# Seven 256-cubed products in place of each 512-cubed product in a two-layer graph network, float32

## The chip, the cores and the metric

The kernel runs on one core of a Trainium2 chip. The metric is the device time of one execution in microseconds (us), the median of several runs. Five engines of the core work side by side, each through its own queue in order: TensorE (PE in the profile, with its weight loads as PEld), VectorE (DVE), ScalarE (ACT), GpSimd (POOL) and SyncE (SP). They meet through semaphores. Sixteen DMA engines move the data.

## The reference

There are 32 independent batches of 512 nodes with 512 features, one adjacency matrix for all, and two layers. Cut to what matters:

```python
# x: (32, 512, 512), adj: (512, 512), all float32
def reference(x, adj, W0, b0, Wq, bq, Wk, bk, Wv, bv, Wo, bo):
    h = jnp.maximum(_layernorm(x), 0.0)
    x = x + jnp.einsum('nm,bmd->bnd', adj, h) @ W0 + b0          # layer 0
    h = jnp.maximum(_layernorm(x), 0.0)                          # layer 1: attention, 8 heads
    q, k, v = heads(h @ Wq + bq), heads(h @ Wk + bk), heads(h @ Wv + bv)
    scores = q @ k.T / 8 + (1.0 - adj) * -1000000000.0
    return x + merge(softmax(scores) @ v) @ Wo + bo
```

The mask term of layer 1 uses a weighted adjacency matrix, so in each row the largest entry of `adj` is ahead of the next by far more than any score. The softmax is then 1 at that place and 0 elsewhere, and the attention is a gather of one row. The kernel tests on the chip whether this holds and takes one of two branches. With the inputs here it takes the gathered branch, `single_path`. That branch needs three 512x512x512 products for each batch: `adj @ h`, then that times `W0`, and `h1 @ (Wv Wo)`; then row `idx[n]` of the last is added to row `n` of `x`.

## The kernel before, in words

A matrix of 512 rows lies in SBUF as 128 partitions by 4 chunks by 512 columns. A TensorE matmul takes a 128x128 block as weights and streams up to 512 columns. One 512-cubed product is 4 output chunks of 4 accumulating matmuls, 128x512 each, into one PSUM bank (pool `ps_m`, 5 banks; pool `ps_t`, 3 banks, is for transposes). In float32 each such matmul leaves two records in the trace, so a product shows as 32 records.

For every batch `b`:

- `ln0(b)` computes the first layer norm and ReLU: VectorE statistics (L163, L164, L166, L170), a power of -0.5 on GpSimd (L168, `rstd`), the scaling with ReLU on ScalarE (L172) into `h0`; GpSimd then adds the bias of layer 0 to `x` (L178).
- `aggregate(b)`, L185: the product of `h0` with the transposed adjacency matrix `adjT`; ScalarE copies it to `yT` (L186).
- `layer0(b)`, L192: the product of `yT` with `w0_s`; VectorE adds it onto `x` (L193), and `norm_relu` makes `h1` from it.
- `layer1(b)`: 16 transposes of `h1` on TensorE (L203), copied by VectorE to `h1T` (L204); the product with the folded weights `wvo` (L208), to which VectorE adds the row `cvo` (L210); the result goes to DRAM as `z` (L211, a DMA issued by ScalarE), an indirect DMA of GpSimd adds the picked rows onto `x` (L213), and SyncE's queue stores `x` (L216).

The outer loop runs `layer0(b)`, `aggregate(b + 1)`, `ln0(b + 2)`, `layer1(b)`. So TensorE's work of one round is 32 records of L192, 32 of L185, 16 transposes and 32 of L208, and while it runs `aggregate(b + 1)` the other engines make `h1` of batch `b`. Nothing in the code fixes the order on an engine: a scheduler of the tile framework places each instruction into its engine's queue ahead of time, and pools (`xpool` 5 batches, `work` 2 buffers a name) decide when a buffer can be written again. A queue is strictly in order at run time.

The folding of the weights (`fold_weights`, L142 to L157) is done once, in the first round. The other branch, `general_path`, is not run with these inputs and is not touched.

Of the kernel before, what the change touches and what calls it, by code (L numbers as in the profile page):

```python
# [8 lines left out]
F32 = mybir.dt.float32  # L9
I32 = mybir.dt.int32  # L10
U32 = mybir.dt.uint32
AF = mybir.ActivationFunctionType
ALU = mybir.AluOpType
AX = mybir.AxisListType
PSUM = bass.MemoryType.PSUM
DRAM = bass.MemoryType.DRAM

P = 128
# [6 lines left out]
def gnn_two_layers(ctx: ExitStack, tc: tile.TileContext, x, adj, w0, b0, wq, bq, wk, bk, wv, bv, wo, bo, out):  # L25
# [66 lines left out]
    with tc.If(single > P - 1) as cmp:  # L92
        single_path(tc, x, w0, b0, wv, bv, wo, bo, out, adjT, idx, ident, ones)
# [3 lines left out]

@with_exitstack
def single_path(ctx: ExitStack, tc: tile.TileContext, x, w0, b0, wv, bv, wo, bo, out, adjT, idx, ident, ones):
    nc = tc.nc  # L100
    B, N, D = x.shape
    C, DC = N // P, D // P

    consts = ctx.enter_context(tc.tile_pool(name="consts", bufs=1))
    xpool = ctx.enter_context(tc.tile_pool(name="xpool", bufs=5 * C))
    work = ctx.enter_context(tc.tile_pool(name="work", bufs=2))
    small = ctx.enter_context(tc.tile_pool(name="small", bufs=4))
    ps_m = ctx.enter_context(tc.tile_pool(name="ps_m", bufs=5, space=PSUM))
    ps_t = ctx.enter_context(tc.tile_pool(name="ps_t", bufs=3, space=PSUM))
    dram = ctx.enter_context(tc.tile_pool(name="dram", bufs=3, space=DRAM))  # L110

    X, H0, YT, H1, Z = {}, {}, {}, {}, {}

    def load_x(b):
        for c in range(C):
            X[b, c] = xpool.tile([P, D], F32, name="x")
            nc.sync.dma_start(X[b, c], x[b, c * P:(c + 1) * P, :])  # L117

    load_x(0)
    w0_s = consts.tile([P, DC, D], F32, name="w0_s")  # L120
    nc.sync.dma_start(w0_s, w0.rearrange("(c p) o -> p c o", p=P))
    b0_r = consts.tile([P, D], F32, name="b0_r")
    nc.gpsimd.dma_start(b0_r, bass.AP(tensor=b0.tensor, offset=b0.offset, ap=[[0, P], [1, D]]))
    load_x(1)
    mhalf = consts.tile([P, C], F32, name="mhalf")
    nc.gpsimd.memset(mhalf, -0.5)
    wvo = consts.tile([P, DC, D], F32, name="wvo")
    cvo = consts.tile([P, D], F32, name="cvo")

    def fold_weights():  # L130
        with ExitStack() as tmp:
            fold = tmp.enter_context(tc.tile_pool(name="fold", bufs=1))
            wv_s = fold.tile([P, DC, D], F32, name="wv_s")
            nc.scalar.dma_start(wv_s, wv.rearrange("(c p) o -> p c o", p=P))
            wo_s = fold.tile([P, DC, D], F32, name="wo_s")
            nc.scalar.dma_start(wo_s, wo.rearrange("(c p) o -> p c o", p=P))
            bv_c = fold.tile([P, DC], F32, name="bv_c")
            nc.gpsimd.dma_start(bv_c, bv.rearrange("(c p) -> p c", p=P))
            nc.gpsimd.dma_start(cvo, bass.AP(tensor=bo.tensor, offset=bo.offset, ap=[[0, P], [1, D]]))
            wvT = fold.tile([P, DC, D], F32, name="wvT")  # L140
            for j in range(DC):
                pt = ps_t.tile([P, DC, P], F32, name="pt")  # L142
                for i in range(DC):
                    nc.tensor.transpose(pt[:, i, :], wv_s[:, i, j * P:(j + 1) * P], ident)  # L144
                nc.scalar.copy(wvT[:, j, :], pt.rearrange("p c q -> p (c q)"))
            for i in range(DC):
                ps = ps_m.tile([P, D], F32, name="mm")
                for j in range(DC):
                    nc.tensor.matmul(ps, wvT[:, j, i * P:(i + 1) * P], wo_s[:, j, :], start=(j == 0), stop=(j == DC - 1))  # L149
                nc.scalar.copy(wvo[:, i, :], ps)  # L150
            part = fold.tile([P, D], F32, name="part")
            nc.vector.tensor_scalar_mul(part, wo_s[:, 0, :], bv_c[:, 0:1])
            for j in range(1, DC):
                nc.vector.scalar_tensor_tensor(part, wo_s[:, j, :], bv_c[:, j:j + 1], part, op0=ALU.mult, op1=ALU.add)
            ps = ps_m.tile([P, D], F32, name="mm")
            nc.tensor.matmul(ps, ones, part, start=True, stop=True)
            nc.vector.tensor_add(cvo, ps, cvo)  # L157

    def norm_relu(b, dst):
        mv = small.tile([P, C, nc.vector.BN_AGGR_DIM], F32, name="mv")  # L160
        for c in range(C):
            st = small.tile([P, nc.vector.BN_STATS_DIM], F32, name="st")
            nc.vector.bn_stats(st, X[b, c])  # L163
            nc.vector.bn_aggr(mv[:, c, :], st)  # L164
        ve = small.tile([P, C], F32, name="ve")
        nc.vector.tensor_scalar_add(ve, mv[:, :, 1], EPS)  # L166
        rstd = small.tile([P, C], F32, name="rstd")
        nc.gpsimd.tensor_tensor(rstd, ve, mhalf, ALU.pow)  # L168
        off = small.tile([P, C], F32, name="off")
        nc.vector.scalar_tensor_tensor(off, mv[:, :, 0], -1.0, rstd, op0=ALU.mult, op1=ALU.mult)  # L170
        for c in range(C):
            nc.scalar.activation(dst[:, c, :], X[b, c], AF.Relu, bias=off[:, c:c + 1], scale=rstd[:, c:c + 1])  # L172

    def ln0(b):
        H0[b] = work.tile([P, C, D], F32, name="h0")
        norm_relu(b, H0[b])
        for c in range(C):
            nc.gpsimd.tensor_add(X[b, c], X[b, c], b0_r)  # L178

    def aggregate(b):  # L180
        YT[b] = work.tile([P, DC, N], F32, name="yT")
        for d in range(DC):
            ps = ps_m.tile([P, N], F32, name="mm")
            for m in range(C):
                nc.tensor.matmul(ps, H0[b][:, m, d * P:(d + 1) * P], adjT[:, m, :], start=(m == 0), stop=(m == C - 1))  # L185
            nc.scalar.copy(YT[b][:, d, :], ps)  # L186

    def layer0(b):
        for c in range(C):
            ps = ps_m.tile([P, D], F32, name="mm")  # L190
            for d in range(DC):
                nc.tensor.matmul(ps, YT[b][:, d, c * P:(c + 1) * P], w0_s[:, d, :], start=(d == 0), stop=(d == DC - 1))  # L192
            nc.vector.tensor_add(X[b, c], ps, X[b, c])  # L193
        H1[b] = work.tile([P, C, D], F32, name="h1")
        norm_relu(b, H1[b])

    def layer1(b):
        h1T = work.tile([P, DC, N], F32, name="h1T")
        Z[b] = dram.tile([N, D], F32, name="z")
        for c in range(C):  # L200
            pt = ps_t.tile([P, DC, P], F32, name="pt")
            for d in range(DC):
                nc.tensor.transpose(pt[:, d, :], H1[b][:, c, d * P:(d + 1) * P], ident)  # L203
            nc.vector.tensor_copy(h1T[:, :, c * P:(c + 1) * P], pt)  # L204
        for c in range(C):
            ps = ps_m.tile([P, D], F32, name="mm")
            for d in range(DC):
                nc.tensor.matmul(ps, h1T[:, d, c * P:(c + 1) * P], wvo[:, d, :], start=(d == 0), stop=(d == DC - 1))  # L208
            zs = work.tile([P, D], F32, name="zs", bufs=C)
            nc.vector.tensor_add(zs, ps, cvo)  # L210
            nc.scalar.dma_start(Z[b][c * P:(c + 1) * P, :], zs)  # L211
        for c in range(C):
            nc.gpsimd.indirect_dma_start(  # L213
                out=X[b, c], out_offset=None, in_=Z[b],
                in_offset=bass.IndirectOffsetOnAxis(ap=idx[:, c, 0:1], axis=0), compute_op=ALU.add)
            nc.sync.dma_start(out[b, c * P:(c + 1) * P, :], X[b, c])  # L216

    ln0(0)
    aggregate(0)
    if B > 1:  # L220
        ln0(1)
    for b in range(B):
        if b + 2 < B:
            load_x(b + 2)
        layer0(b)
        if b == 0:
            fold_weights()
        if b + 1 < B:
            aggregate(b + 1)
        if b + 2 < B:  # L230
            ln0(b + 2)
        layer1(b)
# [265 lines left out]
```

## Time and profile before

| what | us |
|---|---|
| median of 3 runs | 1471.41 (1471.16 to 1471.71) |
| the profiled execution, own time | 1469.63 |
| its span, first to last instruction | 1467.5 |
| TensorE busy in the span | 1407.2 (96%) |
| VectorE busy | 484.4 (33%) |
| GpSimd busy | 430.1 (29%) |
| ScalarE busy | 265.4 (18%) |
| mean granted TensorE clock | 0.991 |

The span is the part of the execution that the profile covers; the 2.1 us between it and the execution's own time lie around it. Busy time of TensorE is a sum over records, which overlap: a record of a 128x512 float32 matmul lasts 0.592 us while the next one starts 0.429 us after it. So the pitch from start to start says how fast the stream runs, and not the duration. The other four engines are busy for a third of the span at most, but a small share of busy time doesn't say whether an engine answers soon enough, nor what stands in front of an instruction in its queue.

### The profile page before, as it was taken

Reading aid. Unit: us, or ns where it says so; the run is one execution under the profiler, and the core shown is the slowest. Engines: PE = TensorE matmul, PEld = TensorE weight load, DVE = VectorE, ACT = ScalarE, POOL = GpSimd, SP = SyncE. Lnnn points to the kernel's source line nnn. Section 1 sums busy time; section 2 is a strip of 40 time slices with the busy share of each in tenths; the row PEclk is TensorE's granted clock in tenths of the full one; section 3 lists DMA queues with packets and bytes.
Section 4 is the critical chain, followed back from the end, with each engine's and each line's share of the span. In section 5 each row is a group of like instructions: output and inputs, shape, how many; then the busy total and the mean of one; then the engine's idle time right before and its main releaser. Section 6 shows DMA issues by size and latency. Waiting matters only on the chain.

```text
span 1467.5 us, 10607 instructions
## 1 busy us (share of the span) xinstructions
PE 1407.2 (96%) x3654; PEld 652.3 (44%) x3654; DVE 484.4 (33%) x1051; ACT 265.4 (18%) x405; POOL 430.1 (29%) x333
## 2 busy tenths in 40 slices
PE   2899999999999999999999999999999999999984
PEld 1344444444444444444444444444444444444441
DVE  2323332333342333333233333323333433333231
ACT  2222102222211222210122221022222112222100
POOL 1313223233323323332322332232333233233111
PEclk9999999999999999999999999999999999999997
DMA  5404432333443234343224344323334422333333
GB/s 175 155 8 108 115 82 79 98 101 101 115 115 72 80 102 105 101 115 100 73 86 107 101 107 115 84 77 98 100 101 115 114 66 88 105 74 72 86 86 89
DMA packets 77216, 141.85 MB, mean 97 GB/s; under 512 B 8416, under 2 KB 8416, under 8 KB 77152
## 3 DMA queue, kind: packets, MB, share of 16 engines
q0 software_dynamic: 18688, 34.09, 15.1%
q1 hardware_dynamic: 37920, 69.22, 13.6%
q10 hardware_dynamic: 20544, 37.76, 6.8%
q8 instruction: 31, 0.51, 0.1%
q14 instruction: 33, 0.27, 0.1%
HBM read 73.93 MB, written 67.11 MB: 96 GB/s over the span
## 4 chain that ended last, share of the span: by engine, by line
PE 95%; DMA 2%; DVE 1%; POOL 0%; ACT 0%; issue 0%; SPq 0%; POOLq 0%; ACTq 0%
PE mm L185 30%; PE mm L208 30%; PE mm L192 30%; PE pt L203 4%; PE mm L149 1%; DMA x<-in_x_dram 1%; DMA wt<-in_L_gnn_Wk_dram 1%; POOL x L213 0%; DVE idx L73 0%; DVE top L72 0%; DMA z<-zs 0%; SPq L117 0%; ACT wt L60 0%; POOLq L493 0%; ACT h L172 0%
## 5 line engine op out<-in xcount | busy, mean ns | idle before, releaser
L185 PE MATMUL mm<-adjT,h 128*128 128x512 f32 x1024 | 446.6, 594 | 7.0 <-ACT h L172 7.0
L208 PE MATMUL mm<-wvo,h1T 128*128 128x512 f32 x1024 | 445.9, 593 | 0.0
L192 PE MATMUL mm<-w_s,yT 128*128 128x512 f32 x1024 | 444.7, 592 | 0.0
L213 POOL DMA_INDIRECT x<-z,idx x128 | 201.0, 1570 | 702.2 <-DMA z<-zs 631.1
L185 PEld LDWEIGHTS mm<-adjT,h 128*128 128x128 f32 x1024 | 195.2, 191 | 253.0 <-issue 238.1
L192 PEld LDWEIGHTS mm<-w_s,yT 128*128 128x128 f32 x1024 | 194.6, 190 | 244.9 <-issue 244.9
L208 PEld LDWEIGHTS mm<-wvo,h1T 128*128 128x128 f32 x1024 | 192.2, 190 | 229.2 <-issue 229.1
L186 ACT COPY yT<-mm 128x512 f32<-128x512 f32 x128 | 74.2, 580 | 1042.2 <-DVE st L163 937.2
L172 ACT ACTIVATE h<-x,off,rstd 128x512 f32<-128x512 f32 x256 | 187.5, 803 | 77.3 <-DVE off L170 74.8
L210 DVE TENSOR_TENSOR zs<-mm,cvo 128x512 f32<-128x512 f32 x128 | 88.5, 691 | 341.0 <-PE mm L208 341.0
L193 DVE TENSOR_TENSOR x<-mm,x 128x512 f32<-128x512 f32 x128 | 88.5, 692 | 269.7 <-PE mm L192 269.7
L163 DVE BATCH_NORM_STATS2 st<-x 128x6 f32<-128x512 f32 x256 | 172.4, 683 | 15.7 <-DMA x<-in_x_dram 11.3
L178 POOL TENSOR_TENSOR x<-x,b_r 128x512 f32<-128x512 f32 x128 | 159.2, 1276 | 52.0 <-ACT h L172 48.3
L204 DVE COPY h1T<-pt 128x512 f32<-128x512 f32 x128 | 79.6, 683 | 250.7 <-PE pt L203 250.7
L168 POOL TENSOR_TENSOR rstd<-ve,mhalf 128x4 f32<-128x4 f32 x64 | 65.5, 1024 | 250.1 <-DVE mv L164 188.5
L203 PE MATMUL pt<-ident,h 128*128 128x128 f32 x512 | 68.1, 276 | 4.3 <-ACT h L172 4.2
L203 PEld LDWEIGHTS pt<-ident,h 128*128 128x128 f32 x512 | 57.9, 142 | 29.3 <-issue 23.3
L164 DVE BATCH_NORM_AGGREGATE mv<-st 128x2 f32<-128x6 f32 x256 | 40.4, 173 | 3.5
L170 DVE SCALAR_TENSOR_TENSOR off<-mv,rstd 128x4 f32<-128x4 f32 x64 | 10.4, 163 | 55.0 <-POOL rstd L168 55.0
L149 PE MATMUL mm<-wo_s,wvT 128*128 128x512 f32 x32 | 13.9, 592 | 0.0
L67 PE MATMUL pt<-ident,mask 128*128 128x128 f32 x16 | 3.9, 426 | 10.0 <-DMA mask<-in_adj_dram 10.0
L144 PE MATMUL pt<-ident,wv_s 128*128 128x128 f32 x16 | 3.6, 423 | 8.3 <-DMA wv_s<-in_L_gnn_Wv_dram 8.3
(44 smaller groups left out, 56.9 us busy)
## 6 DMA issues: line engine op xcount, KB each, us to landing
x<-in_x_dram SPq DMA_DIRECT2D x128, 256.0 KB, 3.5
z<-zs ACTq DMA_DIRECT2D x128, 256.0 KB, 2.0
out_dram<-x SPq DMA_DIRECT2D x128, 256.0 KB, 3.9
x<-z,idx POOLq DMA_INDIRECT x128, 5.9
wt<-in_L_gnn_Wq_dram ACTq DMA_DIRECT2D x1, 1024.0 KB, 9.8
mask<-in_adj_dram SPq DMA_DIRECT2D x1, 1024.0 KB, 9.2
wt<-in_L_gnn_Wk_dram ACTq DMA_DIRECT2D x1, 1024.0 KB, 11.9
wv_s<-in_L_gnn_Wv_dram ACTq DMA_DIRECT2D x1, 1024.0 KB, 7.4
```

The costliest lines, as they stand in the source:

```text
L163: nc.vector.bn_stats(st, X[b, c])
L172: nc.scalar.activation(dst[:, c, :], X[b, c], AF.Relu, bias=off[:, c:c + 1], scale=rstd[:, c:c + 1])
L178: nc.gpsimd.tensor_add(X[b, c], X[b, c], b0_r)
L185: nc.tensor.matmul(ps, H0[b][:, m, d * P:(d + 1) * P], adjT[:, m, :], start=(m == 0), stop=(m == C - 1))
L186: nc.scalar.copy(YT[b][:, d, :], ps)
L192: nc.tensor.matmul(ps, YT[b][:, d, c * P:(c + 1) * P], w0_s[:, d, :], start=(d == 0), stop=(d == DC - 1))
L193: nc.vector.tensor_add(X[b, c], ps, X[b, c])
L203: nc.tensor.transpose(pt[:, d, :], H1[b][:, c, d * P:(d + 1) * P], ident)
L204: nc.vector.tensor_copy(h1T[:, :, c * P:(c + 1) * P], pt)
L208: nc.tensor.matmul(ps, h1T[:, d, c * P:(c + 1) * P], wvo[:, d, :], start=(d == 0), stop=(d == DC - 1))
L210: nc.vector.tensor_add(zs, ps, cvo)
L213: nc.gpsimd.indirect_dma_start(out=X[b, c], out_offset=None, in_=Z[b], in_offset=bass.IndirectOffsetOnAxis(ap=idx[:, c, 0:1], axis=0), com ...
```

## The change

Each of the three products in a batch is computed by Strassen's scheme in Winograd's form. Both operands are seen as 2x2 blocks of 256x256. Instead of 8 block products there are 7, and sums of blocks are formed before and after. The constant operands (`adjT`, `w0_s`, `wvo`) get their four sums once (`sums_b`); the operand that changes with the batch gets them each time (`sums_a`: four additions of 128 partitions by 512 elements). For `h0` they are on GpSimd, for `yT` and `h1T` on VectorE. A block product is 4 matmuls of 128x256 in one PSUM bank (`gemm`); three of the seven stay in the bank `u` and one more in `v`, so that partial sums are accumulated by TensorE, and each of the seven is read by one instruction after it has ended: by VectorE where it is added onto what is there, by ScalarE where it is only copied.

Around this: `aggregate` becomes a generator, and the transposes of `h1`, now a function of their own, are placed after its fourth block product. Their copies go from VectorE to ScalarE. The row `cvo` is no longer added to `z`, but to `x`, four additions on GpSimd in each round. `norm_relu` of layer 0's result is done in two halves. `ps_m` has 6 banks and `ps_t` 2; `work` has one buffer a name but for `h0` and its sums; `xpool` holds 4 batches.

```diff
--- before.py
+++ after.py
@@ -97,24 +97,108 @@
 
 @with_exitstack
 def single_path(ctx: ExitStack, tc: tile.TileContext, x, w0, b0, wv, bv, wo, bo, out, adjT, idx, ident, ones):
     nc = tc.nc
     B, N, D = x.shape
     C, DC = N // P, D // P
+    HALF = N // 2
 
     consts = ctx.enter_context(tc.tile_pool(name="consts", bufs=1))
-    xpool = ctx.enter_context(tc.tile_pool(name="xpool", bufs=5 * C))
-    work = ctx.enter_context(tc.tile_pool(name="work", bufs=2))
+    xpool = ctx.enter_context(tc.tile_pool(name="xpool", bufs=4))
+    work = ctx.enter_context(tc.tile_pool(name="work", bufs=1))
     small = ctx.enter_context(tc.tile_pool(name="small", bufs=4))
-    ps_m = ctx.enter_context(tc.tile_pool(name="ps_m", bufs=5, space=PSUM))
-    ps_t = ctx.enter_context(tc.tile_pool(name="ps_t", bufs=3, space=PSUM))
+    ps_m = ctx.enter_context(tc.tile_pool(name="ps_m", bufs=6, space=PSUM))
+    ps_t = ctx.enter_context(tc.tile_pool(name="ps_t", bufs=2, space=PSUM))
     dram = ctx.enter_context(tc.tile_pool(name="dram", bufs=3, space=DRAM))
 
-    X, H0, YT, H1, Z = {}, {}, {}, {}, {}
+    X, H0, H0S, YT, YTS, H1, H1T, H1TS, Z = {}, {}, {}, {}, {}, {}, {}, {}, {}
 
     def load_x(b):
-        for c in range(C):
-            X[b, c] = xpool.tile([P, D], F32, name="x")
-            nc.sync.dma_start(X[b, c], x[b, c * P:(c + 1) * P, :])
+        X[b] = xpool.tile([P, C, D], F32, name="x")
+        for c in range(C):
+            nc.sync.dma_start(X[b][:, c, :], x[b, c * P:(c + 1) * P, :])
+    def blk(t, chunks, cols):
+        return t[:, 2 * chunks:2 * chunks + 2, cols * HALF:(cols + 1) * HALF]
+    def sums_a(eng, t, name, bufs=1):
+        s = work.tile([P, 4, 2, HALF], F32, name=name, bufs=bufs)
+        a11, a12, a21, a22 = blk(t, 0, 0), blk(t, 1, 0), blk(t, 0, 1), blk(t, 1, 1)
+        eng.tensor_add(s[:, 0], a21, a22)
+        eng.tensor_sub(s[:, 1], s[:, 0], a11)
+        eng.tensor_sub(s[:, 2], a11, a21)
+        eng.tensor_sub(s[:, 3], a12, s[:, 1])
+        return s
+    def sums_b(eng, t, name):
+        s = consts.tile([P, 4, 2, HALF], F32, name=name)
+        b11, b12, b21, b22 = blk(t, 0, 0), blk(t, 0, 1), blk(t, 1, 0), blk(t, 1, 1)
+        eng.tensor_sub(s[:, 0], b12, b11)
+        eng.tensor_sub(s[:, 1], b22, s[:, 0])
+        eng.tensor_sub(s[:, 2], b22, b12)
+        eng.tensor_sub(s[:, 3], b21, s[:, 1])
+        return s
+    def product(a, sa, bt, sb, take):
+        def gemm(bank, lhs, rhs, first):
+            for m in range(2):
+                for k in range(2):
+                    nc.tensor.matmul(bank[:, m, :], lhs[:, k, m * P:(m + 1) * P], rhs[:, k, :],
+                                     start=(first and m == 0 and k == 0), stop=(k == 1), skip_group_check=True)
+        u = ps_m.tile([P, 2, HALF], F32, name="mm")
+        gemm(u, blk(a, 0, 0), blk(bt, 0, 0), True)
+        take("p1", u)
+        yield
+        v = ps_m.tile([P, 2, HALF], F32, name="mm")
+        gemm(v, sa[:, 0], sb[:, 0], True)
+        take("p5", v)
+        yield
+        gemm(u, sa[:, 1], sb[:, 1], False)
+        take("u2", u)
+        yield
+        w = ps_m.tile([P, 2, HALF], F32, name="mm")
+        gemm(w, blk(a, 1, 0), blk(bt, 1, 0), True)
+        take("c11", w)
+        yield
+        gemm(u, sa[:, 2], sb[:, 2], False)
+        take("c22", u)
+        yield
+        gemm(v, sa[:, 3], blk(bt, 1, 1), False)
+        take("c12", v)
+        yield
+        gemm(u, blk(a, 1, 1), sb[:, 3], False)
+        take("c21", u)
+        yield
+    PLACE = {"p1": (0, 0), "p5": (1, 1), "u2": (0, 1), "c11": (0, 0), "c22": (1, 1), "c12": (0, 1), "c21": (1, 0)}
+    def take_new(t):
+        def take(piece, bank):
+            dst = blk(t, *PLACE[piece])
+            if piece in ("c11", "c22", "c12"):
+                nc.vector.tensor_add(dst, bank, dst)
+            else:
+                nc.scalar.copy(dst, bank)
+        return take
+    def take_onto(t):
+        def take(piece, bank):
+            dst = blk(t, *PLACE[piece])
+            nc.vector.tensor_add(dst, bank, dst)
+        return take
 
     load_x(0)
     w0_s = consts.tile([P, DC, D], F32, name="w0_s")
@@ -156,67 +240,72 @@
             nc.tensor.matmul(ps, ones, part, start=True, stop=True)
             nc.vector.tensor_add(cvo, ps, cvo)
 
-    def norm_relu(b, dst):
+    def norm_relu(src, dst, chunks):
...
 
     def ln0(b):
-        H0[b] = work.tile([P, C, D], F32, name="h0")
-        norm_relu(b, H0[b])
-        for c in range(C):
-            nc.gpsimd.tensor_add(X[b, c], X[b, c], b0_r)
+        H0[b] = work.tile([P, C, D], F32, name="h0", bufs=2)
+        norm_relu(X[b], H0[b], range(C))
+        for c in range(C):
+            nc.gpsimd.tensor_add(X[b][:, c, :], X[b][:, c, :], b0_r)
+        H0S[b] = sums_a(nc.gpsimd, H0[b], "h0s", bufs=2)
 
     def aggregate(b):
         YT[b] = work.tile([P, DC, N], F32, name="yT")
-        for d in range(DC):
-            ps = ps_m.tile([P, N], F32, name="mm")
-            for m in range(C):
-                nc.tensor.matmul(ps, H0[b][:, m, d * P:(d + 1) * P], adjT[:, m, :], start=(m == 0), stop=(m == C - 1))
-            nc.scalar.copy(YT[b][:, d, :], ps)
+        yield from product(H0[b], H0S[b], adjT, adjT_s, take_new(YT[b]))
+        YTS[b] = sums_a(nc.vector, YT[b], "yTs")
 
     def layer0(b):
-        for c in range(C):
-            ps = ps_m.tile([P, D], F32, name="mm")
-            for d in range(DC):
-                nc.tensor.matmul(ps, YT[b][:, d, c * P:(c + 1) * P], w0_s[:, d, :], start=(d == 0), stop=(d == DC - 1))
-            nc.vector.tensor_add(X[b, c], ps, X[b, c])
+        for _ in product(YT[b], YTS[b], w0_s, w0_t, take_onto(X[b])):
+            pass
         H1[b] = work.tile([P, C, D], F32, name="h1")
-        norm_relu(b, H1[b])
-    def layer1(b):
-        h1T = work.tile([P, DC, N], F32, name="h1T")
-        Z[b] = dram.tile([N, D], F32, name="z")
+        norm_relu(X[b], H1[b], [0, 1])
+        norm_relu(X[b], H1[b], [2, 3])
+    def transpose_h(b):
+        H1T[b] = work.tile([P, DC, N], F32, name="h1T")
         for c in range(C):
             pt = ps_t.tile([P, DC, P], F32, name="pt")
             for d in range(DC):
                 nc.tensor.transpose(pt[:, d, :], H1[b][:, c, d * P:(d + 1) * P], ident)
-            nc.vector.tensor_copy(h1T[:, :, c * P:(c + 1) * P], pt)
-        for c in range(C):
-            ps = ps_m.tile([P, D], F32, name="mm")
-            for d in range(DC):
-                nc.tensor.matmul(ps, h1T[:, d, c * P:(c + 1) * P], wvo[:, d, :], start=(d == 0), stop=(d == DC - 1))
-            zs = work.tile([P, D], F32, name="zs", bufs=C)
-            nc.vector.tensor_add(zs, ps, cvo)
-            nc.scalar.dma_start(Z[b][c * P:(c + 1) * P, :], zs)
+            nc.scalar.copy(H1T[b][:, :, c * P:(c + 1) * P], pt)
+        H1TS[b] = sums_a(nc.vector, H1T[b], "h1Ts")
+    def layer1(b):
+        for c in range(C):
+            nc.gpsimd.tensor_add(X[b][:, c, :], X[b][:, c, :], cvo)
+        zs = work.tile([P, C, D], F32, name="zs")
+        for _ in product(H1T[b], H1TS[b], wvo, wvo_t, take_new(zs)):
+            pass
+        Z[b] = dram.tile([N, D], F32, name="z")
+        for c in range(C):
+            nc.scalar.dma_start(Z[b][c * P:(c + 1) * P, :], zs[:, c, :])
         for c in range(C):
             nc.gpsimd.indirect_dma_start(
-                out=X[b, c], out_offset=None, in_=Z[b],
+                out=X[b][:, c, :], out_offset=None, in_=Z[b],
                 in_offset=bass.IndirectOffsetOnAxis(ap=idx[:, c, 0:1], axis=0), compute_op=ALU.add)
-            nc.sync.dma_start(out[b, c * P:(c + 1) * P, :], X[b, c])
+            nc.sync.dma_start(out[b, c * P:(c + 1) * P, :], X[b][:, c, :])
+    adjT_s = sums_b(nc.vector, adjT, "adjT_s")
     ln0(0)
-    aggregate(0)
+    w0_t = sums_b(nc.vector, w0_s, "w0_t")
+    for _ in aggregate(0):
+        pass
     if B > 1:
         ln0(1)
     for b in range(B):
@@ -225,8 +314,13 @@
         layer0(b)
         if b == 0:
             fold_weights()
-        if b + 1 < B:
-            aggregate(b + 1)
+            wvo_t = sums_b(nc.vector, wvo, "wvo_t")
+        ahead = aggregate(b + 1) if b + 1 < B else iter(())
+        for _ in range(4):
+            next(ahead, None)
+        transpose_h(b)
+        for _ in ahead:
+            pass
         if b + 2 < B:
             ln0(b + 2)
         layer1(b)
```

The order in which the scheduler places a round's instructions in the built kernel, by queue (`n` marks those of `ln0` of batch `b + 2`; a block product is named by what is read from it, with layer 0 as L0, aggregate as A, layer 1 as L1; s0 to s3 are the four sums):

```
PE    L0: p1 p5 u2 c11 c22 c12 c21 | A: p1 p5 u2 c11 | transposes of chunks 0, 1 | 1 matmul of A c22 |
      transposes of chunks 2, 3 | 3 of A c22, A c12 | 2 of L1 p1 | A c21 | 2 of L1 p1 | L1: p5 u2 c11 c22 c12 c21
DVE   7 additions onto x, mixed with bn_stats of chunks 0 to 3, ve and off of chunks 0, 1, ve and off of chunks 2, 3;
      n bn_stats x4, n ve, n off; add A c11; h1T sums s0 s2 s1; add A c22; h1T sum s3; add A c12;
      yT sums s0 s2 s1 s3; add L1 c11, c22, c12
ACT   copy A p1; ReLU of h1 chunks 0, 1; copy A p5; ReLU of h1 chunks 2, 3; copy A u2; n ReLU x2;
      copy h1T chunks 0, 1; n ReLU; copy h1T chunks 2, 3; n ReLU; copy A c21; copy L1 p1, p5, u2;
      z DMA x2; copy L1 c21; z DMA x2
POOL  indirect DMA x4 of batch b - 1; rstd x2; add cvo x3; n rstd; add cvo; n add b0 x2; h0 sum s2;
      n add b0 x2; h0 sums s0 s1 s3
```

## What the change does to the time, predicted

> **What bounds the kernel now.** I read the chain that ended last first (by engine, then in order of time), then the timeline of one round, then the two places where TensorE does not run evenly: the start and the end.
>
> ```profile
> PE 95%; DMA 2%; DVE 1%; POOL 0%; ACT 0%; issue 0%; SPq 0%; POOLq 0%; ACTq 0%
> PE mm L185 30%; PE mm L208 30%; PE mm L192 30%; PE pt L203 4%; PE mm L149 1%; DMA x<-in_x_dram 1%; DMA wt<-in_L_gnn_Wk_dram 1%; POOL x L213 0%; DVE idx L73 0%; DVE top L72 0%; DMA z<-zs 0%; SPq L117 0%; ACT wt L60 0%; POOLq L493 0%; ACT h L172 0%
> ```
>
> TensorE is the bound. The same chain in order of time shows a round without a gap:
>
> ```profile
> 619.09 1.31 PE pt L203 x12
> 620.40 0.63 PE pt L203 x4
> 621.02 13.74 PE mm L208 x32
> 634.76 13.73 PE mm L192 x32
> 648.49 13.73 PE mm L185 x32
> 662.23 1.31 PE pt L203 x12
> ```
>
> A round is 43.14 us, 32 records are 13.73, so a record has 429 ns; transposes have 109. In this chain layer 0 of batch 1 starts at 117.06 and that of batch 31 at 1411.31, 30 rounds later; 56.2 us follow. TensorE never waits because each other engine is far ahead of it. That must be asked again for the new order.
>
> Two things that decide below show only at the edges. VectorE and GpSimd get in each other's way (timeline of VectorE, then GpSimd):
>
> ```profile
> 39.90 0.75 DVE L154 SCALAR_TENSOR_TENSOR part<-wo_s,bv_c,part 128x512 f32<-128x512 f32 x1
> ...
> 43.90 1.50 DVE L154 SCALAR_TENSOR_TENSOR part<-wo_s,bv_c,part 128x512 f32<-128x512 f32 x1
> ...
> 45.99 1.09 DVE L154 SCALAR_TENSOR_TENSOR part<-wo_s,bv_c,part 128x512 f32<-128x512 f32 x1
> ...
> 47.20 1.02 DVE L166 TENSOR_SCALAR ve<-mv 128x4 f32<-128x4 f32 x1
> ...
> 43.58 5.85 POOL L178 TENSOR_TENSOR x<-x,b_r 128x512 f32<-128x512 f32 x4 [3.65 <-DMA x<-in_x_dram]
> ```
>
> The same instruction takes 0.75 beside no GpSimd addition and 1.50 or 1.09 beside one; `ve`, 0.17 at the median, takes 1.02; and GpSimd's four additions take 5.85 instead of 4.95 (the four of a usual round). And TensorE's clock, by stretches at the end (us of PE busy after the length, PEclk third from the end):
>
> ```profile
> 1426.26:1429.68 3.41, 0.41 (x4) 0.41 (x4) 0.75 (x4) 1.28 (x2) 1.04 (x1) 1.00 0.32 121
> 1429.68:1433.09 3.41, 3.41 (x11) 1.85 (x10) 1.38 (x2) 1.65 (x3) 0.00 (x0) 0.50 0.00 0
> ```
>
> A stretch of 3.41 us with 0.41 of work is followed by one at half the clock.
>
> **What the Trainium skill says.** "SBUF — State Buffer", Who interferes with whom: a VectorE instruction with two SBUF inputs, or in a two-port mode, and a GpSimd instruction that reads SBUF exclude each other for a whole instruction. The trace agrees (0.75 against 1.50). "TensorE: Matmul & The Clock Gate", Part 1: an idle window of about 3.4 us halves the clock until a busy one has passed; the trace agrees (above). Same page, Back-to-back issue gap: N/2.4 + 2.5 ns. A float32 record streams its columns twice, as 2 x 512/2.4 + 2.5 = 429 fits; 128 columns give the 109 of a transpose. "VectorE: DVE Perf Modes", The TRN2 errata: a float32 addition of 512 elements is (512+151)/0.96 = 691 ns, as L193 has it.
>
> **The change part by part.**
> TensorE. A product becomes 28 matmuls of 128x256, 56 records. At 256 columns a record has 213.3 + 2.5 = 215.8 ns, a block product of 8 records 1.727, a product 12.09: 1.65 less than 13.73. Weight loads last 190 ns, below 216, and the one at the last transpose before L208 let its matmul start after 107, so I take no cost; bounds 0 and, if a load should show with 35 ns, 2.0 us a product. A round of pure work is 3 x 12.09 + 16 x 0.109 = 38.00.
>
> Now the new order in one round, t from the start of layer 0. Prices: VectorE 0.69 (0.61 behind an independent one), aggregate 0.12, ve 0.15, off 0.16, rstd 1.02 plus 0.15 before; ScalarE ReLU 0.80 (0.71 in a row), copy 0.58; GpSimd addition 1.27 (1.23 in a row); a reader starts 0.19 after TensorE's slot ends, TensorE 0.10 to 0.13 after its releaser.
>
> 1. TensorE: layer 0 ends at 12.09, the fourth block product of aggregate at 18.99, transposes 0 and 1 at 19.87.
> 2. VectorE adds the seventh product at 12.5 to 13.2; ve of chunks 0, 1 at 14.1; rstd until 15.3; off 15.5; ScalarE's ReLU 0, 1 until 17.0. The next ve stands behind a bn_stats of `ln0`, 16.4; rstd until 17.6.
> 3. GpSimd goes straight to the additions of `cvo`. They are ready, and off of chunks 2, 3 comes 0.05 us later: it is held until 18.8. ReLU 2, 3 until 20.4, the copy of u2 until 20.9. TensorE's single matmul of c22 needs it: wait 1.1.
> 4. VectorE's statistics of `ln0` end in a ve at 20.4, held by the third `cvo` addition until 21.3. Its rstd is queued behind that one on GpSimd: 21.4 to 22.45. Its off is held by the fourth: 23.7.
> 5. On ScalarE the two ReLUs of `ln0` stand ahead of the h1T copies: 23.8 to 25.3, first copy 25.8. With two `ps_t` buffers transposes 2, 3 need that copy. TensorE waits from 21.4 to 25.9: 4.5. The ReLUs are not urgent (that `h0` is used in the next round), but the queue is in order.
> 6. In that wait most rounds have a stretch of 3.41 us with at most 0.43 of work, so half clock follows: up to 1.7.
> 7. h1T's last copy is at 28.4. Sums s0, s2, s1 meet GpSimd's train of eight additions (24.6 to 36): 1.7 each by the alternation seen above, until 33.4, and the addition of A c22 is queued behind them: 34.0. TensorE's A c21 overwrites that bank and waits 1.7.
> 8. Then 0.5 block product of L1, and the rest, without waits: yT's sums end at 38.5, the indirect DMAs (from 3.8, 7.4 long) before rstd is asked for.
>
> Sum 38.0 + 1.1 + 4.5 + 1.7 + up to 1.7 = 47.0; 46.7 as a mean, since the half clock does not fall fully into every round.
>
> The start: aggregate's second block product needs h0's sum s0, six GpSimd additions behind the first ReLU (43.6 + 7.5 + 2 of mutual holds = 53), where before the product ran through; with cold clock its end goes from 59.4 to about 66; from there before took 57.7 to 117.06; three products save 5 and I allow 2.3 of waits. Layer 0 of batch 1: 121 instead of 117.06. The end: 12.09, the same chain as before with one hold, transposes at half clock, 12.09, and the 20.7 from the last L208 record's end (1446.8) to the span's: 55 instead of 56.2.
>
> Span 121 + 30 x 46.7 + 55 = 1577. The execution's own time is 2.1 above its span before (1469.63), the median of runs 1.8 above that (1471.41): 1581; I say 1580.
>
> Edits at nothing: `cvo` moved to GpSimd, 5.1 us a round, is 4 of the additions counted in 3 to 5; the ones on `x` by VectorE instead of 4 are 7 x 0.69 a round, within 1.73 of a block product each. SyncE loads `x` right after the store whose buffer it takes, one round ahead of need; 4 buffers suffice. `work` with one buffer: each is rewritten after its last reader by this order.
>
> **The unknown.** Additions with one input in PSUM never meet a GpSimd addition before. Held: +1.6 a round (48.3, 1629); not held: 0, taken, by the skill. The small off: held (taken), or, if it wins the race, 45.9 (1555).
>
> **Rivals.** Break-even is a round of (1467.5 - 176)/30 = 43.05, 5.05 us above pure work.
> No holds: the pair excludes each other only in long STT forms. For it: just four instructions of before show it. Against: `ve`, the smallest, is among them. Steps 3, 4, 7 shrink: wait 4.3, half clock 1.3, round 43.6: 1488.
> TensorE stays the bound (faster): step 5's wait is what decides. `ln0` waits for nothing of TensorE in this round; if its off came 4 us earlier than worked out, the copies would not wait, the clock would stay, and the round were 38.4: 176 + 30 x 38.4 + 4 = 1332. Between, all below 5.05 us of waits is faster. For it: VectorE is busy only 33% before. Against: its queue is in order and full from 12.5 to 20.5.
> Records of 256 columns limited by weight loads: +35 ns x 168 = 5.9 a round, mostly added: 52, 1740. For it: 190 lies near 216. Against: the 109 ns transposes, with loads of 142.
> That the change isn't what it says is ruled out by the built order, which has 28 such matmuls a product in the branch that ran.
>
> **Numbers.** Forecast (45.5 to 48.3 a round) 0.70, 1545 to 1629, 1580 likeliest. No or partial holds, down to 43.6: 0.18. Faster: 0.06. Weight loads: 0.05. Within 0.2%, about what a measurement of this kernel can tell from none: 0.01. The range 1500 to 1640 leaves out the last cases and the lowest of the partial holds.
>
> **What shows it.** Right: the waits view has TensorE idle for ScalarE's copy of h1T (about 4.5 x 30) and for VectorE's addition onto yT (about 1.7 x 30); record pitch 216 ns; clock mean about 0.96; h1T sums about 1.5 us in the mean against 0.69; a round of 46.7 in the chain. Wrong: pitch above 220, sums at 0.7, or TensorE at 95% of the chain.

## The result, and the profile after

| what | us |
|---|---|
| before, median (4 runs) | 1471.29 (1469.59 to 1471.71) |
| after, median (4 runs) | 1558.35 (1555.88 to 1570.56) |
| ratio | 1.061 (95% interval 1.0555 to 1.0667) |
| after, profiled execution and its span | 1559.11, 1557.3 |
| TensorE busy in the span, mean clock | 1326.1 (85%), 0.942 |

The changed kernel is slower by 6%. TensorE is busy for 81 us less than before (1407.2), and yet the end comes 87 us later. The chain that ended last, by engine and by line, answers to the one shown of the kernel before (TensorE 95%):

```profile
PE 56%; DVE 22%; POOL 12%; ACT 5%; DMA 2%; issue 2%; POOLq 0%; ACTq 0%; SPq 0%; DVEq 0%
```

TensorE no longer sets the end alone. Two lines of the waits view of TensorE (us in total, times, longest us) carry most of it:

```profile
PE pt L284 <- ACT h1T L285: 121.3, 30, 4.1
PE mm L157 <- DVE yT L191: 41.4, 30, 1.9
```

Transposes 2 and 3 wait for ScalarE's copy of h1T in 30 rounds, 4.0 us each, and A c21 for VectorE's addition of A c22, 1.4 us each. The chain in order of time shows the round that starts with layer 0 at 718.54 (start, us, what). TensorE leads until layer 0 ends; then the chain leaves it for 22.5 us, in which TensorE appears only with eight transpose records:

```profile
717.84 11.24 PE mm L157 x52
...
732.59 0.73 POOL rstd L254
...
734.38 0.70 POOL rstd L254
735.08 3.70 POOL x L290 x3
...
738.88 1.03 POOL rstd L254
739.91 0.02 issue
739.94 1.23 DVE off L256
741.17 0.02 issue
741.19 1.52 ACT h L258 x2
742.71 0.48 ACT h1T L285
743.19 0.04 issue
743.23 1.98 PE pt L284 x8
...
745.85 1.72 DVE h1Ts L136
747.58 1.68 DVE h1Ts L138
749.25 1.67 DVE h1Ts L137
750.93 0.61 DVE yT L191
751.54 0.04 issue
751.58 13.43 PE mm L157 x61
```

Read from the end: A c21 starts at 751.58 because the addition of A c22 had to wait for three sums of h1T of 1.7 us; these waited for copies of h1T, these for two ReLUs of the next layer norm, these for a small `off`, this for an rstd, and this for three additions of `cvo` on GpSimd. A p1 started at 730.62, so A c21 comes 20.96 us after it. The TensorE work between the two is 12.95 us (six block products of 1.725, 16 transposes of 0.109, two matmuls of L1). The difference, 8.0, is nearly all that a round has above its work.

The account of the 29 rounds between the layer 0 of batch 1 and that of batch 30, from the starts of TensorE's records: 46.23 us a round, of which 38.02 are records at the usual pitch, 1.93 are records at double pitch (half clock), and 6.27 waits. Start 120.48, last round 38.24, tail 57.97; together 120.48 + 29 x 46.23 + 38.24 + 57.97 = 1557.4.

The last round is a control that the trace holds by itself. In it there is no next layer norm left, and nothing waits. Its TensorE, in one window (length, then busy us and records of PE, PEld, DVE, ACT, POOL, then clock):

```profile
1461.12:1499.35 38.23, 38.23 (x185) 33.42 (x184) 18.18 (x33) 9.55 (x16) 12.60 (x10) 1.00 0.34 84
```

### The profile page after: what moved, and what is told of

Its sections match the earlier page's. It is cut to its first block, busy times and chain, and to the rows that moved or that the text cites. A ratio compares the mean times of both kernels' runs of the same rounds, so it can differ in the third digit from the quotient of the medians.

```text
span 1557.3 us, 16127 instructions
## 1 busy us (share of the span) xinstructions
PE 1326.1 (85%) x5958; PEld 1137.7 (73%) x5958; DVE 868.2 (56%) x1415; ACT 414.0 (27%) x661; POOL 808.4 (52%) x621
## 4 chain that ended last, share of the span: by engine, by line
PE 56%; DVE 22%; POOL 12%; ACT 5%; DMA 2%; issue 2%; POOLq 0%; ACTq 0%; SPq 0%; DVEq 0%
PE mm L157 51%; POOL x L290 7%; POOL rstd L254 5%; DVE st L249 5%; PE pt L284 4%; DVE h1Ts L136 3%; DVE h1Ts L138 3%; DVE h1Ts L137 3%; ACT h L258 3%; DVE off L256 3%; DVE x L199 3%; ACT h1T L285 2%; DVE yT L191 1%; PE mm L233 1%; DMA wt<-in_L_gnn_Wk_dram 1%
## 5 line engine op out<-in xcount | busy, mean ns | idle before, releaser
L157 PE MATMUL mm<-adjT_s,h0s 128*128 128x256 f32 x768 | 215.8, 431 | 5.0 <-POOL h0s L136 5.0
L157 PEld LDWEIGHTS mm<-adjT_s,h0s 128*128 128x128 f32 x768 | 163.6, 221 | 32.1 <-POOL h0s L136 5.8
L157 PE MATMUL mm<-wvo_t,h1Ts 128*128 128x256 f32 x768 | 177.6, 381 | 0.0
L157 PE MATMUL mm<-w_t,yTs 128*128 128x256 f32 x768 | 176.5, 379 | 1.1 <-DVE x L199 1.1
L157 PEld LDWEIGHTS mm<-wvo_t,h1Ts 128*128 128x128 f32 x768 | 147.4, 192 | 20.6
L157 PEld LDWEIGHTS mm<-w_t,yTs 128*128 128x128 f32 x768 | 145.8, 190 | 21.3 <-DVE x L199 1.5
L290 POOL TENSOR_TENSOR x<-x,cvo 128x512 f32<-128x512 f32 x128 | 159.4, 1267 | 0.0
L157 PE MATMUL mm<-wvo,h1T 128*128 128x256 f32 x512 | 130.1, 388 | 0.0
L157 PE MATMUL mm<-adjT,h 128*128 128x256 f32 x512 | 122.8, 383 | 7.5 <-ACT h L258 7.5
L157 PE MATMUL mm<-w_s,yT 128*128 128x256 f32 x512 | 120.9, 379 | 0.0
```

Source lines behind the costliest of these rows:

```text
L157: nc.tensor.matmul(bank[:, m, :], lhs[:, k, m * P:(m + 1) * P], rhs[:, k, :], start=(first and m == 0 and k == 0), stop=(k == 1), skip_gro ...
L290: nc.gpsimd.tensor_add(X[b][:, c, :], X[b][:, c, :], cvo)
```

## The experiments

Theory: a round is 38 us of work plus a chain over the other engines, whose two parts are the order on ScalarE (the ReLUs of the next layer norm ahead of the copies of h1T) and the additions of VectorE and GpSimd that hold each other up. The rivals are that 256-column products, missing PSUM banks or the clock take the time.

### GpSimd's additions left out: e2_no_cvo

```diff
-        for c in range(C):
-            nc.gpsimd.tensor_add(X[b][:, c, :], X[b][:, c, :], cvo)
```

> Leaves out the four additions of cvo to x on GpSimd in each round (cvo is zero with these inputs). Queue theory: the rstd of ln0 no longer stands behind three additions, and off and ve are no longer held by them: 3.7 us of waits ahead of the copy go, of which the wait of the transposes keeps about 2 (VectorE's own queue); the wait of A c21 stays near 1.8, since the eight additions of ln0 still meet the h1T sums. A round of about 42.4, 1450 us. If the holds were nothing and only the queue counted, about 40.2, 1387. Rival, small matmuls: no change, 1558.

Measured 1463.8 us (1462.52 to 1466.01), ratio to the kernel before 0.996 (0.9941 to 0.9975); a round 43.01, with 4.07 of waits and 0.92 of half clock. The waits of TensorE:

```profile
PE mm L157 <- DVE yT L191: 60.8, 29, 2.1
PE pt L284 <- ACT h1T L285: 40.6, 30, 1.4
```

The wait for the copy of h1T falls from 4.0 to 1.4 us, and that for the addition grows from 1.4 to 2.1, since the sums of h1T are still stretched. So the four additions are worth 3.2 us a round, and even without them the Strassen form only draws level. The time is 0.6 us a round above the expected 42.4.

### The sums taken out of GpSimd's way: e3_psum_operand

```diff
+    def sums_p(t, name):
...
+        nc.vector.tensor_add(s[:, 0], fixed, a22)
+        nc.vector.tensor_sub(s[:, 1], s[:, 0], fixed)
+        nc.vector.tensor_sub(s[:, 2], fixed, a21)
+        nc.vector.tensor_sub(s[:, 3], fixed, s[:, 1])
...
-        H1TS[b] = sums_a(nc.vector, H1T[b], "h1Ts")
+        H1TS[b] = sums_p(H1T[b], "h1Ts")
```

The sums of yT are changed likewise. `fixed` is a PSUM bank of zeros that takes the place of one operand, so the sums are not those of the reference.

> The sums of h1T and yT on VectorE read one operand from a fixed PSUM bank of zeros instead of from SBUF (so these sums are not those of the scheme); ps_m has 5 banks. Hold theory: with one SBUF input they are not held by GpSimd's additions, 0.69 us each instead of 1.7, GpSimd's go back from 1.47 to 1.27, and A c21 no longer waits: a round of about 44.4, the wait of the transposes stays at 4.1; 1510 us. Rival (such sums, with their operands in halves, are slow in themselves, 1.7 with or without GpSimd): unchanged, 1558.

Measured 1502.78 us (1501.97 to 1503.22), ratio 1.022 (1.0202 to 1.0236); a round 44.33. One group each of the changed kernel and of this one (busy us, mean ns):

```profile
L138 DVE TENSOR_TENSOR h1Ts<-h1T 128x512 f32<-128x512 f32 x32 | 52.9, 1652 | 0.0
```
```profile
L150 DVE TENSOR_TENSOR h1Ts<-fixed,h1T 128x512 f32<-128x512 f32 x32 | 21.9, 683 | 0.0
```

The sum of 1652 ns takes 683 as soon as one operand lies in PSUM, though GpSimd's additions run beside it as before. The wait of A c21 is gone from the view; that of the transposes stands (121.1 us, 30 times). The holds between the two engines are real, as the Trainium skill has it ("SBUF — State Buffer", Who interferes with whom: two SBUF inputs contend, at most one does not), and those of the sums are worth about 1.9 us a round. This is not the holds quite alone, since the built order changed with them: A c21 stands ahead of the first two matmuls of L1 p1, and VectorE adds A c22 after one sum of h1T instead of three. The second change does not decide: in a round of this run the sums start at 764.77 and A c21 at 768.32, and three sums of 0.68 and the addition would have been over by about 767.5.

### Work put into the wait: e5_filler

```diff
+            if c == 2:
+                for _ in range(4):
+                    nc.tensor.matmul(spare, H1[b][:, 1, 0:P], adjT[:, 0, :], start=True, stop=True)
```

> Four more 128x512 matmuls in each round, 3.4 us of TensorE, into a spare PSUM bank, placed ahead of the transposes of chunks 2 and 3, where TensorE waits 4.1 us; ps_m has 5 banks. Nothing reads their result. Clock theory: the stretch without work is filled, the clock stays at full, and a round gets shorter by 0.5 to 0.9 us although there is more work: 1533 to 1545. If the half clock costs nothing: 1558. If TensorE is short of time after all: up to 3.4 us a round more, 1655.

Measured 1643.66 us (1643.48 to 1644.55), ratio 1.118 (1.1159 to 1.1197); a round 48.94, of which 41.46 work. The expectation missed by 100 us, and this run does not settle what the clock costs (the rounds of the changed kernel and of e2_no_cvo do, in the part on the prediction). The transposes came at full clock, and A c21 started 20.95 us after A p1 as in the changed kernel, so the filler lay wholly inside the wait. But the built order put all of L1 p1 behind A c21 (0.86 us that had lain in the wait), and a new wait stood ahead of it:

```profile
743.37 3.41 PE L159 MATMUL mm<-adjT_s,h 128*128 128x256 f32 x8 [3.75 <-DVE yT L193]
```

Eight records that take 1.9 us take 3.41: half clock, now on records with no wait behind them to absorb the loss. In the round of the changed kernel shown above, the half clock falls on the transposes and on A c22, ahead of A c21, which VectorE's chain holds back in any case.

### Four banks for the transposes: e4_ps_t4

```diff
-    ps_m = ctx.enter_context(tc.tile_pool(name="ps_m", bufs=6, space=PSUM))
-    ps_t = ctx.enter_context(tc.tile_pool(name="ps_t", bufs=2, space=PSUM))
+    ps_m = ctx.enter_context(tc.tile_pool(name="ps_m", bufs=4, space=PSUM))
+    ps_t = ctx.enter_context(tc.tile_pool(name="ps_t", bufs=4, space=PSUM))
```

> Four PSUM banks for the transposes and four for the products, in place of two and six. Transposes 2 and 3 then need no bank that ScalarE must first copy out, so their wait of 4.1 us goes; nothing else of the chain is touched (the copies still stand behind the ReLUs, the sums of h1T behind the copies, A c21's bank behind the sums). Theory A (the order on ScalarE is the cause, the transposes only show it): the wait moves to A c21, L1 p1 or L1 p5, which then wait 4 to 6 us for the copy or for the addition on VectorE, and the round stays at 45 to 47 us: 1530 to 1575. Rival B (the missing transpose banks are the cause): the round falls by the 4.1 us to 42 us, 1432.

Measured 1602.52 us (1600.84 to 1603.16), ratio 1.089 (1.0873 to 1.0909); a round 47.80, above the range of both. In the timeline:

```profile
761.13 1.91 PE L284 MATMUL pt<-ident,h 128*128 128x128 f32 x16
...
764.80 1.52 ACT L258 ACTIVATE h<-x,off,rstd 128x512 f32<-128x512 f32 x2 [2.84 <-DVE off L256]
...
766.23 2.02 ACT L285 COPY h1T<-pt 128x512 f32<-128x512 f32 x4
...
773.94 3.78 PE L157 MATMUL mm<-adjT_s,h 128*128 128x256 f32 x8 [7.44 <-DVE yT L191]
```

The 16 transposes run in one piece, and the copies still stand behind the two ReLUs. The wait moved to A c21, as theory A has it: 7.44 us in place of 4.1 and 1.4. That the round is 1.6 longer has the reasons of e5_filler: all of L1 p1 now stands behind A c21 (0.86), and A c21 runs at half clock (3.78 in place of 1.99). Against these, the chain got a little shorter: A c21 starts 19.71 us after A p1 (754.23), in place of 20.96. So the banks, with the order that came with them, were worth 1.25 us of the chain, but they are not the cause of the 4.1 us.

### The next layer norm asked for first: e1_ln0_first and e7_ln0_first_x5

```diff
         if b + 2 < B:
             load_x(b + 2)
+            ln0(b + 2)
         layer0(b)
...
-        if b + 2 < B:
-            ln0(b + 2)
```

> The call of ln0 for batch b + 2 stands ahead of layer0(b) in the program. In the built order one thing of a round changes: the four ReLUs of that ln0 stand behind the copies of h1T on ScalarE, not ahead of them. Queue theory (the transposes wait because the copy is queued behind ReLUs that wait for GpSimd): the 4.1 us wait of the transposes goes, the half clock goes with it, the 1.85 us wait of A c21 shrinks to about 0.6 as GpSimd's additions come later; a round of about 39.4 us instead of 46.1, and 29 rounds of it give about 1365 us. Rival, the small matmuls: if the 128x256 records or their weight loads are what costs, the order changes nothing, 1558. Rival, the clock alone: the half clock costs at most 1.7 of a round, so 1510 at best.

Measured 1564.02 us (1561.9 to 1569.75), ratio 1.063 (1.0612 to 1.0647): no gain, and the expectation missed by 200 us. The order on ScalarE did become the wished one, but the layer norm done within a round is now that of one batch further, whose `x` is not there yet:

```profile
702.13 1.96 SPq L127 DMA_DIRECT2D x<-in_x_dram  x4
...
704.68 0.69 DVE L249 BATCH_NORM_STATS2 st<-x 128x6 f32<-128x512 f32 x1 [5.68 <-DMA x<-in_x_dram]
...
709.54 1.22 PE L157 MATMUL mm<-adjT_s,h0s 128*128 128x256 f32 x2 [5.62 <-ACT yT L193]
```

VectorE's statistics wait 5.68 us for the load, which waits for a buffer; behind them in the queue stands the `off` of h1, behind that ReLU and the copy of A u2, and TensorE waits 5.62 us for that. If this is so, a fifth buffer of `x` must bring the whole gain:

```diff
-    xpool = ctx.enter_context(tc.tile_pool(name="xpool", bufs=4))
+    xpool = ctx.enter_context(tc.tile_pool(name="xpool", bufs=5))
```

> The order of e1_ln0_first (the layer norm of the next batch asked for at the top of the round) with five x buffers in place of four. If what took the gain of e1_ln0_first was the load of x, which found its buffer still held by a store not yet out, the wait of bn_stats for the load (7.9 us, 33 times) is gone, A c22 finds the copy of u2 in time, and the round is 39 to 41 us: 120 + 29 x 40 + 38 + 58 = 1376 us (1350 to 1410). If the load was not the cause, it stays at 1550 to 1570.

Measured 1354.55 us (1353.99 to 1355.68), ratio 0.921 (0.9197 to 0.9228); a round 39.15. The wait for the load falls from 180.6 us to 6.7 in the whole execution (waits view of e1_ln0_first, then of e7_ln0_first_x5):

```profile
DVE st L249 <- DMA x<-in_x_dram: 180.6, 33, 7.9
DVE st L249 <- DMA x<-in_x_dram: 6.7, 3, 4.4
```

The idea of e1_ln0_first was right, and it had only traded one wait for another.

### One buffer for h0: e6_h0_one

The cleanest form of the question: nothing is moved in the code.

```diff
-        H0[b] = work.tile([P, C, D], F32, name="h0", bufs=2)
+        H0[b] = work.tile([P, C, D], F32, name="h0", bufs=1)
```

The built order changes little but for ScalarE: the four ReLUs of the next layer norm stand behind the copies of h1T and of A c21. In the steady rounds VectorE and GpSimd keep their order, and TensorE's differs only in how the matmuls of L1 are interleaved.

> One buffer for h0 in place of two, nothing else. The four ReLUs of the next layer norm on ScalarE can then only start when the aggregate's last product has read the old h0, so they come behind the copies of h1T and of the last yT block, and nothing is left out or added. Theory A (the round's 46.2 us are 38.2 of work and a chain: transposes 2 and 3 wait 4.1 us for ScalarE behind two ReLUs, the additions of h1T on VectorE then run beside GpSimd's and are stretched, A c21 waits for the addition behind them, and the wait brings half clock): the wait of transposes 2 and 3 for the h1T copy falls from 4.1 us to under 0.5, the additions on line 136 from 1.6 to about 1 us on the mean, half clock is nearly gone (mean clock over 0.98), a round takes 39.9 to 40.9 us, and the whole 120.5 + 29 x 40.4 + 38.2 + 58 = 1388 us (1365 to 1405), below the kernel before's 1471. The new waits are then about 1 us at A c21 and about 1 us at L1 u2, whose bank waits for a copy behind the four ReLUs. Rival B (what the round costs above its work is the contention of VectorE with GpSimd, wherever ScalarE's queue stands): the same additions are stretched in another place, the round is 44 to 46 us and the whole 1500 to 1560. Rival C (256-column products themselves, or the clock, take it): no change, 1545 to 1570.

Measured 1354.07 us (1353.31 to 1354.73), ratio 0.921 (0.919 to 0.9221). One line, and the kernel goes from 6% slower to 8% faster than the one before. A round in the timeline, to be laid beside the chain of the changed kernel above (A p1 starts at 717.93):

```profile
725.57 1.07 ACT L285 COPY h1T<-pt 128x512 f32<-128x512 f32 x2
...
726.26 1.09 PE L284 MATMUL pt<-ident,h 128*128 128x128 f32 x8
...
727.25 1.23 DVE L256 SCALAR_TENSOR_TENSOR off<-mv,rstd 128x4 f32<-128x4 f32 x1 [1.13 <-POOL rstd L254]
...
729.00 0.68 DVE L136 TENSOR_TENSOR h1Ts<-h1T 128x512 f32<-128x512 f32 x1
...
731.53 1.99 PE L157 MATMUL mm<-adjT_s,h 128*128 128x256 f32 x8 [0.73 <-DVE yT L191]
...
734.05 2.93 ACT L258 ACTIVATE h<-x,off,rstd 128x512 f32<-128x512 f32 x4
...
734.94 2.82 POOL L264 TENSOR_TENSOR x<-x,b_r 128x512 f32<-128x512 f32 x2 [6.48 <-ACT h L258]
```

The copies no longer wait, so transposes 2 and 3 follow at once. A c21 comes 13.60 us after A p1 in place of 20.96. And the second part of the chain goes with the first: the ReLUs now come at 734.05, GpSimd's additions of `b0` and the sums of h0 only after them, and the sums of h1T, done by then, take 0.68 each, where three of the four took 1.6 and the last 1.1. A round is 39.26: 38.02 of work, 1.24 of waits, no half clock. Theory A named both effects and put the round at 40.4, so it still asked for 1.1 us too many; rivals B and C fall.

### The row cvo added on VectorE: e8_h0_one_cvo_z

e6_h0_one with the four additions of `cvo` off GpSimd:

```diff
             if piece in ("c11", "c22", "c12"):
                 nc.vector.tensor_add(dst, bank, dst)
+            elif row is not None:
+                cols = PLACE[piece][1]
+                nc.vector.tensor_add(dst, bank, row[:, None, cols * HALF:(cols + 1) * HALF].to_broadcast([P, 2, HALF]))
             else:
                 nc.scalar.copy(dst, bank)
...
-        for c in range(C):
-            nc.gpsimd.tensor_add(X[b][:, c, :], X[b][:, c, :], cvo)
...
-        for _ in product(H1T[b], H1TS[b], wvo, wvo_t, take_new(zs)):
+        for _ in product(H1T[b], H1TS[b], wvo, wvo_t, take_new(zs, cvo)):
```

> e6_h0_one with the four additions of cvo taken off GpSimd: ScalarE's four copies of the last product's blocks out of PSUM become VectorE additions of PSUM and the row cvo (each row of z is gathered once per row of the output, so the sum is the same). Theory A: GpSimd is 5.0 us emptier in the stretch where off, ve and the sums of h1T run, the off of chunks 2 and 3 takes 0.16 us again, L1 u2 no longer waits for a copy behind the ReLUs, the VectorE additions fall into its idle microseconds between products. A round of 38.3 to 39.6 us: 120.5 + 29 x 38.9 + 38.2 + 58 = 1345 us (1325 to 1370), 1 to 2 us per round below e6_h0_one. Rival B: the additions of b0 and of h0, moved to the end of the round, stretch the sums of yT on VectorE, which now stand in front of the four new additions, and the round is 41 us or more: 1406 us or more, no gain over e6_h0_one.

Measured 1319.34 us (1318.69 to 1319.57), ratio 0.897 (0.8955 to 0.8985). That is 6 us below the expected range: a round is 38.11, within 0.1 of the work alone. The chain is TensorE's again:

```profile
PE 94%; DMA 3%; DVE 1%; POOL 1%; issue 0%; ACT 0%; POOLq 0%; SPq 0%; ACTq 0%
```

This version beats both kernels, and what is left of a round is the work itself.

### The same buffer in the kernel before: e9_before_h0_one

`bufs=1` for `h0` in the kernel before, nothing else.

> The kernel before with one buffer for h0, nothing else; a control for e6_h0_one. Theory A (the gain of e6_h0_one lies in the order around the Strassen form; the kernel before is held by TensorE's 44 us a round): no gain, 1466 to 1480; the ReLUs start some us later, behind the last aggregate product, and nothing on TensorE waits for them. Rival B (the kernel before carried the same fault, and its one-buffer form would be the fair one to compare with): 1440 or below.

Measured 1470.11 us (1468.68 to 1471.06), ratio 0.9995 (0.9986 to 1.0004). The kernel before had no such fault: on its engines the order stays as it was, and the gain of the buffer belongs to the new form.

## Why the prediction was right, step by step

It said 1580 us with 1500 to 1640 and slower at 0.93; measured 1558.35. The mechanism is the predicted one, but for the part that half clock has in it (step 6). For the round that starts at 718.54, in us from there:

| step | predicted | measured |
|---|---|---|
| pitch of a block product | 1.727 | 1.725 |
| 1: layer 0 ends; transposes 0, 1 start | 12.09; 18.99 | 12.08; 18.99 |
| 2: ReLU 0, 1 end | 17.0 | 16.5 |
| 3: copy of u2 ends; wait of A c22 | 20.9; 1.1 | 19.8; none |
| 4: second off ends | 23.7 | 22.6 |
| 5: first copy of h1T ends; wait of transposes 2, 3 | 25.8; 4.5 | 24.6; 4.12 (mean 4.0) |
| 6: half clock | up to 1.7 | mean 1.93 |
| 7: sums s0, s2, s1 end; wait of A c21 | 33.4; 1.7 | 32.4; 1.01 (mean 1.4) |
| round, mean | 46.7 | 46.23 |

Step 2 comes 0.5 us earlier than predicted, and all from step 3 on about 1 us. The term at fault is the rstd: it was taken as 1.02, which is the duration of 128x4; the two halves of `norm_relu` have 128x2, and these take 0.71 (groups of the changed kernel, mean ns after the busy time):

```profile
L254 POOL TENSOR_TENSOR rstd<-ve,mhalf 128x2 f32<-128x2 f32 x64 | 45.2, 707 | 120.0 <-DVE ve L252 120.0
L254 POOL TENSOR_TENSOR rstd<-ve,mhalf 128x4 f32<-128x4 f32 x32 | 32.6, 1020 | 16.3 <-DVE ve L252 13.2
```

Two of them make 0.6 of it; the rest lies in smaller terms, such as a hand-over from ve to rstd of 0.09 in place of 0.15. With it the wait of step 3 vanished. In the sum of the round, the waits of steps 3, 5 and 7 are 5.4 in place of 7.3, the half clock is 1.93 in place of 1.4 in the mean, and 0.85 lies in gaps of 0.05 to 0.17 around each stop, which the prediction did not count. So the predicted round was 0.47 too long, which over 29 rounds makes 14 us of the 20 by which the span of 1577 misses 1557.3. A further 8.5 is the last round: the prediction counted 30 equal rounds, but the last has no layer norm of a next batch, and so takes 38.24 in place of 46.7. Against these stand the tail, 57.97 in place of 55 (3.0 too short), and the start, 120.48 in place of 121 (0.5).

In step 6 the sum came right for a partly wrong reason, which is luck. The prediction expected half clock in most rounds, after stretches with at most 0.43 us of work. It came in all 29, with 1.4 to 3.1 us of it in each, and about half of the times after a busier stretch (last section). The mean clock was 0.942, lower than the 0.96 named as a sign.

Nor does half clock ahead of A c21 lengthen a round. By the times of steps 5 and 7, TensorE at full clock would have reached A c21 at about 30.7 and waited 3.4 us there; the 1.7 of step 7 is what is left of this when half clock has taken 1.7. The two share one stretch, which ends with VectorE's addition, so a round with less half clock waits longer. The 0.3 that the prediction took off for such rounds (47.0 to 46.7) had no ground. The trace has both kinds side by side. Of the rounds that start at 718.54 and 764.64, one has 2.21 us of half clock and the other 1.36, and they take 46.10 and 46.09. The wait of A c21 makes up the difference:

```profile
751.58 1.99 PE L157 MATMUL mm<-adjT_s,h 128*128 128x256 f32 x8 [1.01 <-DVE yT L191]
797.68 1.99 PE L157 MATMUL mm<-adjT_s,h 128*128 128x256 f32 x8 [1.86 <-DVE yT L191]
```

Half clock costs time where it falls on A c21 and the records behind it. That is so in the last three of the 29 rounds (47.8 each), and in 17 rounds of e2_no_cvo, which take 43.71 where the other 12 take 42.02: 1.7 us.

The unknowns: additions of PSUM and SBUF are not held by GpSimd (the addition at 750.93 in the chain takes its usual 0.68 in the timeline while a GpSimd addition runs, and e3_psum_operand), and the small `off` is held wherever the prediction had it held, in 31 of 32 batches for chunks 2, 3 and in 29 of 32 for the next layer norm (1.22; that of chunks 0, 1 takes 0.16). Both had been taken so.

The rivals: "no holds" falls with e3_psum_operand; "weight loads limit 256-column records" with the pitch; "TensorE stays the bound" named the right switch, step 5's wait. It asked for an `off` 4 us earlier, which was not needed: the ReLUs had only to stand behind the copies. It gave 1332 and 38.4 a round; e6_h0_one has 1354 and 39.26, and e8_h0_one_cvo_z 1319 and 38.11.

What the parts are worth, each taken alone from 46.23 a round: the order on ScalarE 7.0 (e6_h0_one), the `cvo` additions 3.2 (e2_no_cvo), the holds of the two sets of sums 1.9 (e3_psum_operand, with its changes of order). Together that is more than the 8.2 above the work, since the order also ends the holds on the sums.

## What to carry to other kernels

When TensorE's work is cut, price the chain over the other engines from one TensorE wait to the next before counting the gain: here 5 us less work a round freed nothing, because an instruction with a whole round of slack stood in a strict queue ahead of a copy with none. A buffer count is also an order: one buffer more let the unhurried ReLUs start early, one less put them where they belong. When a wait is removed and no time comes back, look for what is late next (the load in e1_ln0_first, A c21 in e4_ps_t4) before the idea is dropped.

## What the runs showed of the hardware that was not expected

Half clock does not need a nearly idle stretch. The prediction knew one of 3.41 us with 0.41 of work. In e2_no_cvo two waits of TensorE for VectorE, both of 2.1 us, fall differently onto the stretches at whose ends the clock is set (PE busy after the length, clock third from the end):

```profile
703.37:706.78 3.41, 1.30 (x7) 0.83 (x6) 3.41 (x4) 0.00 (x0) 3.33 (x3) 1.00 0.00 0
706.78:710.20 3.42, 3.42 (x10) 2.71 (x9) 3.39 (x4) 0.59 (x1) 2.93 (x2) 0.50 0.00 0
747.74:751.15 3.41, 1.48 (x7) 1.32 (x8) 3.41 (x4) 0.00 (x0) 3.33 (x3) 1.00 0.02 5
751.15:754.57 3.42, 3.42 (x18) 3.01 (x17) 3.39 (x4) 1.45 (x3) 2.27 (x2) 1.00 0.00 0
```

Here a stretch busy for 1.30 us (38%) is followed by half clock, and one busy for 1.48 (43%) is not. The stretches run on a fixed grid, as the Trainium skill says ("TensorE: Matmul & The Clock Gate", Part 1: the window is free-running): 703.37 and 747.74 lie 13 stretches of 3.413 apart. So the same wait of 2.1 us brings half clock in 17 of the 29 rounds and not in the others. The runs show no sharp limit between the two: in the changed kernel half clock followed a stretch with 1.47 us of work (1396.61 to 1400.02), and in e1_ln0_first it did not follow one with 1.44 (1520.71 to 1524.12).

An instruction of 128x4 elements, `off`, takes 1.22 us in place of 0.16 when it starts (at 739.94 in the changed kernel) 0.06 us after a GpSimd addition of 1.25; with the additions of `cvo` left out (e2_no_cvo) it takes 0.16 throughout. So here a hold was as long as what was left of the holding instruction, however small the held one.
